# Low sums and the small products among them as two column halves of the TensorE array

## The chip, the cores and the metric

The kernel runs on one NeuronCore of a Trainium2 chip. The metric is the device time of one execution in microseconds; each time given for a kernel is a median over several runs. A profile is one execution recorded by the hardware profiler: every instruction of every engine has its start and duration, and the waits between engines are inferred from semaphores. The engines are named PE (TensorE matmuls), PEld (TensorE weight loads), DVE (VectorE), ACT (ScalarE), POOL (GpSimd) and SP (SyncE, which issues most transfers).

## The reference

One block of a perceiver: cross attention of 32 x 64 queries on 32 contexts of 1601 keys, then a recurrent mixing of the 64 positions, then a feed-forward layer, each on the layer-normed input and each added to it. All in float32.

```python
def xattn(query, context, w_q, w_kv, w_out, b_out):      # 16 heads of 64
    q = query @ w_q                                      # 256 -> 1024
    k, v = split(context @ w_kv)                         # 192 -> 2 x 1024
    attn = softmax(q k^T * 64**-0.5)                     # per head, 64 x 1601
    return (attn v) @ w_out + b_out

def mixing(x, ...):
    k, v, r = k_in @ Wk.T, v_in @ Wv.T, sigmoid(r_in @ Wr.T)   # inputs mixed with the shifted x
    wkv = scan over time of (num + e*v) / (den + e)
    return (r * wkv) @ Wo.T + bo

x = x + xattn(layernorm(x), ctx_768, ...)
x = x + mixing(layernorm(x), ...)
x = x + relu(layernorm(x) @ w1 + b1) @ w2 + b2           # 256 -> 1024 -> 256
```

## The kernel before, in words

**Folding.** The key and value weights are never applied to the context. In a setup part (up to about 140 us) the queries are multiplied by the key weights, so that a score is a product of 192 context channels with a folded query; the folded queries go through DRAM (`q_dram`). The value weights are applied after the sums over the keys (`Out.vproj`). A context of 1601 keys is 12 chunks of 128 keys and one of 65 (`KC` = 12, `KR` = 65, `NCK` = 13), and has 192 channels: 128 "low" ones and 64 "high" ones (`C2` = 64).

**Halves.** The attention loop runs over `u` = 0 to 63: 32 contexts, each with two halves of 8 heads (8 x 64 = 512 columns, `HALF`). For each half PE does, in this order:

- `scores(u)`: for each chunk three products with 64 channels each (L466), where the chunks go in pairs: one uses array rows 0 to 63, the other rows 64 to 127, so that two matmuls of 64 rows x 128 columns run at once (row pairs). The last chunk's 65 keys are done in L485, with 256 moving columns a matmul.
- `av_lo` of the half before (`last`): the low sums. 13 matmuls (L569) with the 128 low channels of a chunk as the weights (128 rows x 128 columns, the whole array) and the 512 columns of exponentials as the moving operand, all added in one PSUM tile `o_lo`. After some of the chunks a list `fill` puts in other work:
  - phase 1 (every fourth half): `Out.yproj` after chunk 2 (8 matmuls, L642, tile `y_ps`, 256 moving columns) and `Mixing.out` of an earlier tile after chunk 6 (2 matmuls, L444, `ry`);
  - phase 2: `Mixing.mix` after chunk 6, with two 128 x 128 transposes on PE (L361, `xT_ln`);
  - phase 3: `Mixing.project` after chunk 3 (Wk and Wv, four matmuls each, L383 in `proj`) and `Mixing.gate` after chunk 9 (Wr, four more).
- `Out.vproj` in phase 0: value weights, 64 columns a matmul (L629, `v_ps`), two heads in the two column halves of the array.
- `av_hi`: the high sums. The weights are the 64 high channels of a chunk, so a matmul needs 64 columns of the array; even chunks use columns 0 to 63 and odd ones columns 64 to 127, and their sums stay apart in the two partition halves of `o_hi` (12 matmuls in L583, two more for the 65 keys in L593, with 256 moving columns each). Which column half a matmul uses follows from the partitions of its output: `self.ph[o * C2 : (o + 1) * C2, :]`.

A matmul in float32 leaves two records in the trace, each with a weight load of its own, so 832 matmuls of the low sums (64 halves x 13) are 1664 records.

Meanwhile ACT copies scores out of PSUM (L473) and takes exponentials (L514), DVE takes maxima (L477), subtracts them (L513), adds the exponentials up (L540) and transposes the next context (L260), and POOL reduces over partitions (L503, L546). No planner sets the order: PE executes its instructions as the loop issues them.

**After the loop** the last half's sums are done with `older.project` and `older.gate` as fill, then `vproj`, `yproj`, and the feed-forward part: transposes of the normed rows (L749), `h_ps` (L761) and `fy` (L775) over four blocks of 512 rows, all with the whole array. Among the first two blocks' matmuls stand the rest of the last two mixing tiles: `older.out` (L444), `mixer.mix` (L361), `mixer.project` and `mixer.gate` (L383), `mixer.out` (L444).

Of the kernel before, what the change touches and what calls it, by code (L numbers as in the profile page):

```python
# [15 lines left out]
P = 128  # L16
# [4 lines left out]
def kernel(  # L21
# [35 lines left out]
    nc = tc.nc  # L57
# [59 lines left out]
    with ExitStack() as st_b:  # L117
        with ExitStack() as st_a:
# [218 lines left out]
            ps_s = st_a.enter_context(tc.tile_pool(name="ps_s", bufs=2, space=PSUM))  # L337
            ps_o = st_a.enter_context(tc.tile_pool(name="ps_o", bufs=1, space=PSUM))

            def bank(shape, name):  # L340
                return ps_m.tile(shape, F32, tag="m", name=name)

            class Mixing:
# [13 lines left out]
                def mix(self):  # L357
                    i = self.i
                    pt = bank([P, 2, 2, T], f"xT_ln2_{i}")
                    for c in range(2):  # L360
                        nc.tensor.transpose(pt[:, c, :, :], self.xn[:, c * P : (c + 1) * P], ident)  # L361
                    xp = rp.tile([P, 2, 2, T + 1], F32, tag="xp", name=f"xp_{i}")
                    nc.gpsimd.memset(xp[:, :, :, 0:1], 0.0)
                    nc.scalar.copy(xp[:, :, :, 1 : T + 1], pt)
                    self.mixed = []
                    for n, nm in enumerate(("k", "v", "r")):
                        tmp = rp.tile([P, 2, 2, T], F32, tag="e", name=f"tmp_{nm}_{i}")
                        mi = rp.tile([P, 2, 2, T], F32, tag=f"in_{nm}", name=f"in_{nm}_{i}")
                        for c in range(2):
                            nc.scalar.activation(  # L370
                                tmp[:, c], xp[:, c, :, 0:T], AF.Copy, scale=omm[:, n, c : c + 1]
                            )
                            nc.vector.scalar_tensor_tensor(
                                mi[:, c], xp[:, c, :, 1 : T + 1], cols[:, 2 + n, c : c + 1],
                                tmp[:, c], ALU.mult, ALU.add,
                            )
                        self.mixed.append(mi.rearrange("p c b t -> p c (b t)"))

                def proj(self, n, w):
                    ps = bank([P, 2, 2, T], f"{w}_ps_{self.i}")  # L380
                    for c in range(2):
                        for hc in range(2):
                            nc.tensor.matmul(  # L383
                                ps[:, c, :, :],
                                lhsT=rw_T[w][:, hc, c * P : (c + 1) * P],
                                rhs=self.mixed[n][:, hc, :],
                                start=(hc == 0),
                                stop=(hc == 1),
                            )
                    return ps  # L390
# [49 lines left out]
                def out(self):  # L440
                    i = self.i
                    py = bank([P, D], f"ry_{i}")
                    for c in range(2):
                        nc.tensor.matmul(  # L444
                            py,
                            lhsT=self.rw[:, c, :],
                            rhs=rw_T["Wo"][:, c, :],
                            start=(c == 0),
                            stop=(c == 1),
                        )  # L450
                    nc.vector.tensor_tensor(x_sb[:, i, :], x_sb[:, i, :], py, ALU.add)
                    nc.vector.tensor_tensor(
                        x_sb[:, i, :], x_sb[:, i, :], bias_rows[:, 1, :], ALU.add
                    )
# [65 lines left out]
            class Half:  # L520
# [43 lines left out]
                def av_lo(self, fill):  # L564

                    self.po = ps_o.tile([P, HALF], F32, tag="o_lo", name=f"o_lo_{self.u}")
                    for c in range(NCK):
                        n = P if c < KC else KR
                        nc.tensor.matmul(  # L569
                            self.po,  # L570
                            lhsT=self.ctx[0:n, self.at[c], 0:P],
                            rhs=self.s_sb[0:n, c, :],
                            start=(c == 0),
                            stop=(c == NCK - 1),
                        )
                        for work in fill.get(c, ()):
                            work()
# [36 lines left out]
            class Out:  # L614
# [23 lines left out]
                def yproj(self):  # L638
                    i = self.i
                    py = bank([P, D], f"y_ps_{i}")  # L640
                    for k in range(NP):
                        nc.tensor.matmul(  # L642
                            py,
                            lhsT=self.outT[:, k, :],
                            rhs=wo_sb[:, k, :],
                            start=(k == 0),
                            stop=(k == NP - 1),
                        )
                    nc.vector.tensor_tensor(x_sb[:, i, :], x_sb[:, i, :], py, ALU.add)
                    nc.vector.tensor_tensor(  # L650
                        x_sb[:, i, :], x_sb[:, i, :], bias_rows[:, 0, :], ALU.add
                    )
# [5 lines left out]
            for u in range(2 * B):  # L658
                b, j = divmod(u, 2)

                phase, i = (u - 5) % 4, (u - 5) // 4
                out, mixer, older = outs[max(i, 0)], mixers[max(i, 0)], mixers[max(i - 1, 0)]
                fill = {}
                if phase == 1 and i >= 0:
# [46 lines left out]
            older, mixer, out = mixers[NT - 2], mixers[NT - 1], outs[NT - 1]  # L711
# [138 lines left out]
```

## Time and profile before

| | |
|---|---|
| median of 3 runs | 2626.44 us (2626.01 to 2626.71) |
| the profiled execution, its own time | 2624.3 us |
| its span | 2622.5 us |
| granted TensorE clock, mean | 0.997 |
| PE busy | 2593.2 us, 99% |
| DVE busy | 1907.2 us, 73% |
| ACT busy | 953.6 us, 36% |
| DMA, mean share of the 16 engines in queue q1 | 32.9% |
| attention loop, low sums first at | 186 us, last at 2485 us |

How to read the profile's lines: a group is a line of the kernel, an engine and an operation, the tiles "out<-in", the rows*columns of the array and partitions x moving columns of the operand, the number of records, then busy time in all, mean ns of one, and the idle time ahead of them. Matmuls are pipelined: a record lasts longer than the distance to the next one, so busy time of a group divided by its count, or the distance of starts, tells the rate, not the mean duration. In a timeline a line gives start, duration, engine, line, operation and the number of records merged in it.

### The profile page before, as it was taken

The page shows a single profiled execution, that of the slowest core. Times are in us where ns is not written, and L with a number is a line of the kernel's source. Part 1 is how long each engine was busy: PE and PEld are TensorE (multiplying, and loading weights), DVE is VectorE, ACT ScalarE, POOL GpSimd, SP SyncE. Part 2 cuts the span into 40 slices and gives each one's busy share as a digit, 9 for nine tenths or more (in the row PEclk, how much of TensorE's full clock was granted, in tenths as well). Part 3 has the DMA queues.
Part 4 walks back from the last instruction along what each step waited for, and adds up shares of the span by engine and source line. Part 5 has one row for each costly group of instructions (what it writes and reads, how often), then busy time and mean ns, then how long its engine had stood idle before and what let it go on. Part 6 is the DMA issues. An engine that isn't in the chain of part 4 may idle for free.

```text
span 2622.5 us, 28521 instructions
## 1 busy us (share of the span) xinstructions
PE 2593.2 (99%) x11456; PEld 1217.1 (46%) x11456; DVE 1907.2 (73%) x2283; ACT 953.6 (36%) x1019; POOL 355.3 (14%) x176
## 2 busy tenths in 40 slices
PE   8989999999999999999999999999999999999999
PEld 3334444444444444444444444444444444444466
DVE  4458878777787878777787868777787868787741
ACT  2333334333333334343433333343433334343221
POOL 0011111111111111111111111111111111111100
PEclk9989999999999999999999999999999999999999
DMA  8983333233322323333331313333331323310100
GB/s 202 284 162 57 56 51 63 44 63 63 63 57 49 63 39 63 44 63 63 63 63 44 63 39 63 46 61 63 63 63 44 63 45 57 59 29 20 51 11 23
DMA packets 437781, 169.33 MB, mean 65 GB/s; under 512 B 332400, under 2 KB 423952, under 8 KB 437648
## 3 DMA queue, kind: packets, MB, share of 16 engines
q1 hardware_dynamic: 437104, 166.46, 32.9%
q8 instruction: 90, 1.47, 0.3%
q10 hardware_dynamic: 544, 1.05, 0.1%
q14 instruction: 43, 0.35, 0.0%
HBM read 138.60 MB, written 27.26 MB: 63 GB/s over the span
## 4 chain that ended last, share of the span: by engine, by line
PE 96%; DMA 2%; SPq 1%; DVE 1%; POOL 0%; issue 0%; ACT 0%; DVEq 0%; POOLq 0%; ACTq 0%
PE s_ps L466 37%; PE o_lo L569 28%; PE o_hi L583 13%; PE s_ps_r L485 3%; PE fy L775 2%; PE v_ps L629 2%; PE y_ps L642 2%; PE h_ps L761 2%; PE q_ps L195 2%; PE o_hi L593 1%; PE ql_ps L211 1%; DMA q_dram<-q_lo 1%; PE Wv_ps L383 1%; PE Wr_ps L383 1%; PE Wk_ps L383 1%; DMA q_dram<-q_hi 1%
## 5 line engine op out<-in xcount | busy, mean ns | idle before, releaser
L466 PE MATMUL s_ps<-q,cT 64*128 64x512 f32 x4608 | 1011.3, 594 | 8.6 <-ACT s_sb L473 7.8
L569 PE MATMUL o_lo<-s_sb,c 128*128 128x512 f32 (+1 forms) x1664 | 743.5, 596 | 0.0
L473 ACT COPY s_sb<-s_ps 128x1024 f32<-128x1024 f32 x384 | 388.6, 1012 | 958.6 <-PE s_ps L466 945.5
L466 PEld LDWEIGHTS s_ps<-q,cT 64*128 64x128 f32 x4608 | 442.6, 188 | 548.9 <-issue 537.9
L514 ACT ACTIVATE s_sb<-s_sb 128x2048 f32<-128x2048 f32 (+1 forms) x256 | 398.6, 1585 | 466.0 <-DVE s_sb L513 466.0
L513 DVE TENSOR_TENSOR s_sb<-s_sb,mb 128x2048 f32<-128x2048 f32 (+1 forms) x256 | 471.6, 1886 | 101.9 <-POOL mb L503 101.9
L569 PEld LDWEIGHTS o_lo<-s_sb,c 128*128 128x128 f32 (+1 forms) x1664 | 307.5, 190 | 358.1 <-issue 350.8
L477 DVE TENSOR_TENSOR m<-m,s_sb 128x1024 f32<-128x1024 f32 x256 | 313.6, 1225 | 180.1 <-ACT s_sb L473 168.2
L583 PE MATMUL o_hi<-s_sb,c 128*64 128x512 f32 x1536 | 342.9, 595 | 0.0
L546 POOL PARTITION_ALL_REDUCE den<-sum x64 | 207.4, 3240 | 834.9 <-DVE oT L609 673.2
L540 DVE TENSOR_TENSOR t<-t,s_sb 128x1024 f32<-128x1024 f32 x256 | 310.5, 1213 | 4.0
L503 POOL PARTITION_ALL_REDUCE mb<-mx x64 | 114.2, 1785 | 906.7 <-DVE mx L496 788.7
L583 PEld LDWEIGHTS o_hi<-s_sb,c 128*64 128x64 f32 x1536 | 105.3, 137 | 220.0 <-issue 197.2
L556 DVE STREAM_TRANSPOSE turned<-den 128x512 f32<-128x512 f32 x64 | 45.5, 711 | 221.3 <-POOL den L546 221.3
L485 PE MATMUL s_ps_r<-q,cT 64*65 64x256 f32 x768 | 93.6, 376 | 0.0
L260 DVE STREAM_TRANSPOSE cT<-cb 128x768 f32<-128x768 f32 x96 | 92.7, 967 | 0.0
L475 DVE TENSOR_TENSOR m<-s_sb 128x1024 f32<-128x1024 f32 x64 | 75.8, 1184 | 10.3 <-ACT s_sb L473 10.3
L485 PEld LDWEIGHTS s_ps_r<-q,cT 64*65 64x65 f32 x768 | 54.0, 134 | 52.8 <-issue 33.5
L538 DVE TENSOR_TENSOR t<-s_sb 128x1024 f32<-128x1024 f32 x64 | 77.5, 1211 | 0.0
L102 POOL TENSOR_TENSOR rstd_ln<-rstd_ln,root 128x1 f32<-128x1 f32 (+1 forms) x24 | 31.3, 1304 | 276.5 <-DVE rstd_ln L101 276.5
L195 PE MATMUL q_ps<-xnT,wq_sb 128*128 128x512 f32 x128 | 61.0, 616 | 0.0
L642 PE MATMUL y_ps<-wo_sb,outT 128*128 128x256 f32 x256 | 58.0, 379 | 0.0
(111 smaller groups left out, 1507.4 us busy)
## 6 DMA issues: line engine op xcount, KB each, us to landing
q<-q_dram SPq DMA_DIRECT2D x64, 768.0 KB, 6.6
c<-in_ctx_dram SPq DMA_DIRECT2D x32, 1152.0 KB, 6.2
cb<-in_ctx_dram SPq DMA_DIRECT2D x192, 104.0 KB, 4.2
cb<-in_ctx_dram SPq DMA_DIRECT2D x192, 96.0 KB, 3.3
q_dram<-q_lo SPq DMA_DIRECT2D x16, 1024.0 KB, 8.6
q_dram<-q_hi SPq DMA_DIRECT2D x32, 256.0 KB, 6.8
x_sb<-in_x_dram SPq DMA_DIRECT2D x4, 512.0 KB, 9.7
w_sb<-in_L_ffn_w_dram SPq DMA_DIRECT2D x2, 1024.0 KB, 5.0
```

The lines of the kernel that those rows point to most:

```text
L195: nc.tensor.matmul(pq, lhsT=wq_sb[:, c, hp * P : (hp + 1) * P], rhs=xnT[:, c, :], start=(c == 0), stop=(c == 1),)
L466: nc.tensor.matmul(ps[:, k, :], lhsT=cT[rs, s, i * P : (i + 1) * P], rhs=q[rs, s, js : js + HALF], start=(s == 0), stop=(s == NS - 1),)
L473: nc.scalar.copy(s_sb[:, 2 * i : 2 * i + 2, :], ps)
L477: nc.vector.tensor_tensor(m2, m2, s_sb[:, 2 * i : 2 * i + 2, :], ALU.max)
L485: nc.tensor.matmul(ps[0:KR, k, 0:HH], lhsT=cT[rs, s, NB1 * BL : KT + 1], rhs=q[rs, s, js + k * HH : js + (k + 1) * HH], start=(s == 0), st ...
L503: nc.gpsimd.partition_all_reduce(mb, mx, P, bass_isa.ReduceOp.max)
L513: nc.vector.tensor_tensor(s, s, m, ALU.subtract)
L514: nc.scalar.activation(s, s, AF.Exp)
L540: nc.vector.tensor_tensor(t2, t2, p[:, 2 * i : 2 * i + 2, :], ALU.add)
L546: nc.gpsimd.partition_all_reduce(self.den, self.sum, P, bass_isa.ReduceOp.add)
L569: nc.tensor.matmul(self.po, lhsT=self.ctx[0:n, self.at[c], 0:P], rhs=self.s_sb[0:n, c, :], start=(c == 0), stop=(c == NCK - 1),)
L583: nc.tensor.matmul(self.ph[o * C2 : (o + 1) * C2, :], lhsT=self.ctx[:, self.at[c], P:C], rhs=self.s_sb[:, c, :], start=(c < 2), stop=False ...
```

## The change

A helper beside `bank` in the attention part splits one matmul of 128 output partitions in two of 64: the same moving operand, half of the weights' columns each, and the two partition halves of the same output.

```diff
+            def matmul(out, lhsT, rhs, start, stop):
+
+                for o in range(2):
+                    rs = slice(o * P // 2, (o + 1) * P // 2)
+                    nc.tensor.matmul(
+                        out[rs], lhsT=lhsT[:, rs], rhs=rhs, start=start, stop=stop,
+                        skip_group_check=True,
+                    )
```

It is called in place of `nc.tensor.matmul` in four places, with nothing else changed there:

```diff
 (Mixing.proj, L383)
-                            nc.tensor.matmul(
+                            matmul(
                                 ps[:, c, :, :],
 (Mixing.out, L444)
-                        nc.tensor.matmul(
+                        matmul(
                             py,
 (Half.av_lo, L569)
-                        nc.tensor.matmul(
+                        matmul(
                             self.po,
 (Out.yproj, L642)
-                        nc.tensor.matmul(
+                        matmul(
                             py,
```

The transposes, the scores, `vproj`, the high sums and the feed-forward matmuls stay as they are.

## The prediction

> **What bounds the kernel now.** I read the page's busy shares, clock row and chain first.
>
> ```profile
> PE 2593.2 (99%) x11456; PEld 1217.1 (46%) x11456; DVE 1907.2 (73%) x2283; ACT 953.6 (36%) x1019; POOL 355.3 (14%) x176
> ...
> PEclk9989999999999999999999999999999999999999
> ...
> PE 96%; DMA 2%; SPq 1%; DVE 1%; POOL 0%; issue 0%; ACT 0%; DVEq 0%; POOLq 0%; ACTq 0%
> ```
>
> TensorE is busy nearly throughout at its full granted clock, and 96% of the chain that ended last is PE. In the view of the waits all of PE's waits add to 24.4 us, and none lies between 180 and 2474 us. So in the attention loop time leaves the span only where PE's own records come closer together; VectorE, the next engine, has 27% to spare.
>
> Next the groups by line, with shapes kept apart.
>
> ```profile
> L569 PE MATMUL o_lo<-s_sb,c 128*128 128x512 f32 x1536 | 688.5, 597 | 0.0
> ...
> L583 PE MATMUL o_hi<-s_sb,c 128*64 128x512 f32 x1536 | 342.9, 595 | 0.0
> ```
>
> The low sums (L569) use all 128 columns and take 688.5 / 1536 = 448 ns a record. The high sums (L583) use 64 columns, two matmuls in the two column halves at once: 342.9 / 1536 = 223 ns a record, 446 a pair. Each matmul of the program leaves two records (64 halves x 13 = 832 matmuls, 1664 records of L569). So whole array and column pair already work at one rate. Inside a run the starts are 429 ns apart for both; a pair's second record starts 7 ns after its first. Column tiles therefore promise nothing in steady state; the question is the seams. Three arrangements follow each other in every half: row pairs (scores, L466 and L485), whole array (L569 and what is put among it), column pairs (L629, L583, L593). The timeline shows the seam from whole to columns:
>
> ```profile
> 1288.98 0.19 PEld L569 LDWEIGHTS o_lo<-s_sb,c 65*128 65x128 f32 x1 [0.24 <-issue]
> 1289.41 0.19 PEld L569 LDWEIGHTS o_lo<-s_sb,c 65*128 65x128 f32 x1 [0.24 <-issue]
> 1290.36 0.20 PEld L583 LDWEIGHTS o_hi<-s_sb,c 128*64 128x64 f32 x4 [0.76 <-issue]
> ...
> 1290.84 0.14 PEld L583 LDWEIGHTS o_hi<-s_sb,c 128*64 128x64 f32 x2 [0.29 <-issue]
> ```
>
> Within a run a load goes out beside the matmul before it, every 0.43. At the seam it doesn't: the last low record starts at 1289.84, so the next was due at 1290.27, but load and matmul come together at 1290.36 (0.09 late), and the second pair comes 0.48 instead of 0.43 later (0.05, the first load of 64 columns that nothing covers). The record starts give 91 + 51 = 142 ns; all 64 ends of low sums (49 into L583, 15 into L629) lie within 1 ns of each part. The seam from row pairs to whole:
>
> ```profile
> 1278.47 0.38 PE L485 MATMUL s_ps_r<-q,cT 64*65 64x256 f32 x2
> 1278.78 0.70 PE L569 MATMUL o_lo<-s_sb,c 128*128 128x512 f32 x1
> ...
> 1279.32 0.19 PEld L569 LDWEIGHTS o_lo<-s_sb,c 128*128 128x128 f32 x1 [0.24 <-issue]
> ```
>
> L485's pairs are 0.216 apart, so 1278.68 was due: 0.10 late, and the next start is 0.53 instead of 0.43 later, 0.10 for a load of 128 columns. The records: 98 + 104 ns, 63 times. Where the arrangement stays, the seam is free even if line and tile change:
>
> ```profile
> 1217.58 0.39 PE L629 MATMUL v_ps<-oT,wv_hi 128*64 128x128 f32 x4
> 1217.80 0.60 PE L583 MATMUL o_hi<-s_sb,c 128*64 128x512 f32 x2
> ```
>
> Four records of L629 are two pairs of 109 ns, and 0.22 is just that. So are L569 into L642 and back. A switch from columns to whole happens once in the loop's end, from L593 into L569 at 2470.98: 99 + 104.
>
> **The change, part by part.** It makes column pairs of L569, L383, L444 and L642. The transposes of mix (L361) and everything in the feed-forward part stay whole. Arithmetic, transfers, waits and order stay; each of 1664 + 256 + 384 + 64 = 2368 records becomes a pair, two matmuls and two loads more in place of one and one.
>
> 1. The end of the low sums no longer changes arrangement: 64 x 142 ns = 9.09 us less.
> 2. Their beginning goes from row pairs to column pairs, a seam that the trace lacks. The gap is 91 to 99 ns at every clean switch, whichever two arrangements meet (columns to rows 98, whole to columns 91), so I leave its 98. The uncovered load is 51 for 64 columns and 104 for 128; here it is 64, so 53 ns less: 63 x 53 = 3.34 us. If the load stayed at 104, nothing.
> 3. L593 into L569 at 2470.98 (203 ns) and L629 into L642 at 2494.25 (100 + 105) vanish: 0.41 us.
> 4. L383's records are loads of 128 columns with 128 moving columns. From 1316.58 to 1318.36 sixteen take 1.78 us, 111.3 each; L629's pairs, the same work in halves, 3.06 us for 28 (1214.74 to 1217.80), 109.3. 384 x 2.0 = 0.77 us less, bounded by none and by this.
> 5. L642 and L444 move 256 columns at 216 ns. As pairs: L485's pairs take 216, L593's 220. I take 216, since the 4 ns of L593 also stand in L569 whole where its rows go from 128 to 65 (433 for 429); at 220 it would be 320 x 4 = 1.3 us more.
> 6. Mix's two transposes stand among low sums in 15 halves (1284.89 is one), now with no seam. They get two: columns to whole, 98 + 55 (a transpose's load, from 133.38, where L320 follows L226), and back, 91 + 51. 15 x 295 ns = 4.43 us more; between 55 and 104 for that load it is up to 0.74 more.
> 7. In the feed-forward part L444 (twice), L383 (two places) stand among whole-array work, and the transposes L749 follow L642. Nine switches: 153, 142, 153, 142, 202, 142, 204, 142 and 202 ns, 1.48 us. The first three (448 ns) lie ahead of L361 at 2504.64, where PE waits 1.39 us for VectorE's `xn_ln`, which hangs on L642 and not on them; that cover takes them, or costs 0.45 if it is gone. 1.03 us more.
>
> PE's sequencer gets more instructions: a pair has four where there were two. L629 issues four in every 109 ns with no gap, and the densest new run, L383, needs the same, so I count none. The Trainium skill ("TensorEngine Tiling (Array Packing)", section "Instruction Overhead") speaks against this, giving each matmul some 60 cycles of overhead; at the 2.4 GHz of its page "TensorE: Matmul & The Clock Gate" 2368 further records in series would be an estimated 59 us more. L629's rows contradict a cost in series.
>
> The sum: 9.09 + 3.34 + 0.41 + 0.77 - 4.43 - 1.03 = 8.15 us less. PE waits for nobody in the loop, so all of it should reach the end; a cycle shrinks by some 0.2 us in 34, and the ACT copies of L473 idle 1.56 us before each, so nothing is late next. The profiled execution took 2624.3 us (span 2622.5); it would be 2616.2. The runs' median is 2.1 above it: 2626.44 - 8.1 = **2618.3 us**, 0.31% less. A measurement of this kernel tells about 0.2% (5.25 us) from no change.
>
> **Rivals.**
>
> - *A pair with one moving operand isn't free.* The halves of L583 read different chunks and those of L629 different heads; the new halves read the same columns at the same moment, which no row shows. If only the 7 ns by which the second starts later added to each pair, 2368 x 7 = 16.6 us more, 2634.9 us, slower. It eats the gain from 3.4 ns a pair, and is slower by over 0.2% from 5.6. If halves ran one after another it would be 1664 x 429 + 384 x 111 + 320 x 216 ns, some 826 us. Against it: 429 ns is the start distance of pair and whole record alike, so the 7 ns are hidden there. Chance 0.11. The Trainium skill ("TensorE: Matmul & The Clock Gate", section "Measured speedup vs the span model") adds about 4 ns per further tile to a pack's span: an estimated 9.5 us more here, 2627.8; the rows of L583 show no such sum in a run of packs.
> - *The entry from row pairs keeps its price* (104 ns, or a longer gap as both directions change), or the switches round mix cost more than the rows. Without step 2 it is 4.8 us less: 2621.6, which is within 0.2%. For it: no row has this seam. Against it: the load's price goes by its columns at every seam seen. Chance 0.15.
> - *The change doesn't do what it says*: the switch into the high sums stays, because the tiles meet there in another way. Without step 1, 0.9 us more: 2627.4. Against it: L629 into L583 is free and its tiles are those of L569 then. Chance 0.09.
>
> **How the numbers follow.** The forecast has 0.65. Range: below, the tail's switches all hidden and a median apart by the runs' 0.7 us, 2616.5; above, step 2 lost (3.3), step 5 at 220 (1.3) and part of steps 4, 6 and 7, 2623.5. That holds the forecast and the second rival, 0.80. Faster by over 0.2%: 0.65 and a third of the second rival, 0.70. Within: the rest of that, the third rival and a mild first, 0.20. Slower: the first, 0.10.
>
> **What would show it.** L583 after L569 with its load 0.43 after the one before and no 0.09; the first low pair 0.31 after L485's last and the next 0.48 later; L569 with twice the records at 223 ns each and loads of 137 ns; about 0.15 before and after L361. Pairs of L569 at 433 or more would prove the first rival; wrong too would be any new wait of PE.

## The result, and the profile after

The changed kernel takes 2616.94 us (median of 6 runs, 2615.43 to 2618.07), the kernel before 2626.55 us beside it; the ratio of the runs is 0.9965 (the two medians alone give 0.9963), 95% interval 0.9955 to 0.9976, so 6.3 to 11.8 us faster. Run again beside other kernels it came out at 0.9965 (0.9953 to 0.9978). The forecast was 2618.3 us, 0.31% less.

The page of after (span 2616.2 us; its own time 2618.07), the same lines as before:

```profile
PE 2588.2 (99%) x13824; PEld 1129.4 (43%) x13824; DVE 1908.3 (73%) x2283; ACT 953.6 (36%) x1019; POOL 356.4 (14%) x176
...
PEclk9989999999999999999999999999999999999999
...
PE 95%; DMA 2%; DVE 1%; SPq 1%; issue 0%; POOL 0%; ACT 0%; DVEq 0%; POOLq 0%; ACTq 0%
```

Nothing has changed hands: PE is still the bound, at the same clock, with 2368 more records (11456 to 13824). The groups by line, shapes apart (the helper's calls all have L344; L583 is now L592):

```profile
L344 PE MATMUL o_lo<-s_sb,c 128*64 128x512 f32 x3072 | 686.6, 595 | 0.0
L592 PE MATMUL o_hi<-s_sb,c 128*64 128x512 f32 x1536 | 340.4, 592 | 0.0
```

686.6 / 3072 is 223.5 ns a record, 447 a pair: the low sums cost in halves what they cost whole (448). The gain stands at their ends. The timeline at the end of the low sums of one half (start, duration, line; PEld are the loads, each beside the matmul before its own):

```profile
591.63 0.14 PEld L344 LDWEIGHTS o_lo<-s_sb,c 65*64 65x64 f32 x2 [0.29 <-issue]
592.07 0.14 PEld L592 LDWEIGHTS o_hi<-s_sb,c 128*64 128x64 f32 x2 [0.29 <-issue]
...
592.50 0.14 PEld L592 LDWEIGHTS o_hi<-s_sb,c 128*64 128x64 f32 x2 [0.29 <-issue]
...
592.93 0.14 PEld L592 LDWEIGHTS o_hi<-s_sb,c 128*64 128x64 f32 x2 [0.29 <-issue]
```

L592's first loads go out beside the last low matmul, and everything is 0.43 apart: the seam is gone. The entry:

```profile
505.40 0.81 PE L494 MATMUL s_ps_r<-q,cT 64*65 64x256 f32 x6
...
506.14 0.20 PEld L344 LDWEIGHTS o_lo<-s_sb,c 128*64 128x64 f32 x4 [0.38 <-issue]
...
506.62 0.14 PEld L344 LDWEIGHTS o_lo<-s_sb,c 128*64 128x64 f32 x2 [0.28 <-issue]
```

Three pairs of 0.216 from 505.40 end at 506.05, so 506.14 is still 0.09 to 0.10 late, but the next start is 0.48 later and no longer 0.53. Where mix's two transposes stand, both switches are new:

```profile
842.13 1.03 PE L344 MATMUL o_lo<-s_sb,c 128*64 128x512 f32 x4
843.09 0.44 PE L370 MATMUL xT_ln<-ident,xn_ln 128*128 128x128 f32 x2
843.46 0.65 PE L344 MATMUL o_lo<-s_sb,c 128*64 128x512 f32 x2
```

Two pairs of 0.43 from 842.13 end at 842.99, and L370 comes 0.10 after that; its two records, 0.22 without seams, hold PE for 0.37.

One measure is used from here on: the time from the first record of the low sums to the end of the span. It is 2436.09 us before (first record at 186.44) and 2428.26 after (187.98): 7.83 us less. The profile of after_again, the same kernel, gives 2428.27, so it repeats far better than the whole time. The part ahead of it executes the same instructions in both kernels, yet in ten profiles the first low sum comes between 185.0 and 191.1 us, in no order by kernel.

### The profile page after: what moved, and what is told of

The parts are those of the page before. It is cut to its first block, busy times and chain, and to the rows that moved or that the text cites. A ratio compares the mean times of both kernels' runs of the same rounds, so it can differ in the third digit from the quotient of the medians.

```text
span 2616.2 us, 33242 instructions
## 1 busy us (share of the span) xinstructions
PE 2588.2 (99%) x13824; PEld 1129.4 (43%) x13824; DVE 1908.3 (73%) x2283; ACT 953.6 (36%) x1019; POOL 356.4 (14%) x176
## 4 chain that ended last, share of the span: by engine, by line
PE 95%; DMA 2%; DVE 1%; SPq 1%; issue 0%; POOL 0%; ACT 0%; DVEq 0%; POOLq 0%; ACTq 0%
PE s_ps L475 38%; PE o_lo L344 28%; PE o_hi L592 13%; PE s_ps_r L494 3%; PE fy L784 2%; PE v_ps L638 2%; PE h_ps L770 2%; PE y_ps L344 2%; PE q_ps L195 1%; DMA q_dram<-q_lo 1%; PE o_hi L602 1%; PE Wk_ps L344 1%; PE Wr_ps L344 1%; PE Wv_ps L344 1%; PE ry L344 1%; SPq L242 0%
## 5 line engine op out<-in xcount | busy, mean ns | idle before, releaser
L475 PE MATMUL s_ps<-q,cT 64*128 64x512 f32 x4608 | 1010.3, 594 | 8.0 <-ACT s_sb L482 7.1
L344 PE MATMUL o_lo<-s_sb,c 128*64 128x512 f32 (+1 forms) x3328 | 741.6, 594 | 0.0
L475 PEld LDWEIGHTS s_ps<-q,cT 64*128 64x128 f32 x4608 | 442.2, 188 | 547.6 <-issue 537.9
L344 PEld LDWEIGHTS o_lo<-s_sb,c 128*64 128x64 f32 (+1 forms) x3328 | 231.1, 137 | 427.4 <-issue 417.7
L592 PE MATMUL o_hi<-s_sb,c 128*64 128x512 f32 x1536 | 340.4, 592 | 0.0
L592 PEld LDWEIGHTS o_hi<-s_sb,c 128*64 128x64 f32 x1536 | 109.3, 136 | 211.3 <-issue 206.1
L344 PE MATMUL y_ps<-wo_sb,outT 128*64 128x256 f32 x512 | 58.0, 379 | 0.0
```

Source lines behind the costliest of these rows:

```text
L344: nc.tensor.matmul(out[rs], lhsT=lhsT[:, rs], rhs=rhs, start=start, stop=stop, skip_group_check=True,)
L475: nc.tensor.matmul(ps[:, k, :], lhsT=cT[rs, s, i * P : (i + 1) * P], rhs=q[rs, s, js : js + HALF], start=(s == 0), stop=(s == NS - 1),)
L592: nc.tensor.matmul(self.ph[o * C2 : (o + 1) * C2, :], lhsT=self.ctx[:, self.at[c], P:C], rhs=self.s_sb[:, c, :], start=(c < 2), stop=False ...
```

## The experiments

| kernel | median us | ratio to before (95%) | first low sum to end: expected, measured |
|---|---|---|---|
| lo_only | 2637.97 | 1.0046 (1.0031 to 1.0061) | 2448.5, 2448.39 |
| small_only | 2646.7 | 1.0081 (1.0067 to 1.0095) | 2457.2, 2457.03 |
| mix_at_entry | 2614.05 | 0.9958 (0.9945 to 0.9970) | 2426, 2426.04 |
| rest_first | 2614.99 | 0.9961 (0.9949 to 0.9974) | 2425.1, 2425.74 |
| tail_whole | 2616.76 | 0.9967 (0.9954 to 0.9979) | 2426.9, 2426.98 |
| all_three | 2610.52 | 0.9945 (0.9932 to 0.9957) | 2421.4 to 2422.2, 2421.96 |
| quarters | 2625.99 | 0.9998 (0.9989 to 1.0007) | 2436 to 2438, 2435.96 |
| after_again | 2616.8 | 0.9965 (0.9953 to 0.9978) | 2428.2, 2428.27 |

The theory is that of the seams. Its main rival is that column tiles are cheaper in themselves, whatever stands around them; the first two kernels undo one part of the change each.

### lo_only: the low sums alone

```diff
 (Mixing.proj, Mixing.out, Out.yproj)
-                            matmul(
+                            nc.tensor.matmul(
```

> Only the low sums in column halves; the small products stay whole. Theory of seams (each change of arrangement costs a gap of 91 to 101 ns and one uncovered load: 51 ns for 64 columns, 104 for 128, 55 for a transpose; inside a run column pairs and whole array go at 429 ns): the gains of steps 1 to 3 stay without the last product's seam (-12.6 us), mix costs 15 x 302 ns = +4.5, and the small products among the low sums are 59 excursions (15 of the output projection, 14 + 30 of the mixing products) of 101 + 104 + 92 + 51 = 347 ns = +20.5. Against before +12.4 us, about 2639, slower by 0.47%; from the first low sum to the end of the span 2448.5 us (before 2436.1, after 2428.2). Rival, column tiles are cheaper in themselves (shorter loads, 137 for 190 ns) and what stands around them doesn't matter: the low sums are 1664 of the 2368 records, so about 70% of the gain of after, -5 to -7 us, about 2620.

It is slower than before. The last gate product of a half, whole again (L392) between low sums in halves:

```profile
886.01 1.46 PE L344 MATMUL o_lo<-s_sb,c 128*64 128x512 f32 x6
887.40 1.16 PE L392 MATMUL Wr_ps<-in_r,Wr_T 128*128 128x128 f32 x8
888.49 1.51 PE L344 MATMUL o_lo<-s_sb,c 128*64 128x512 f32 x6
```

Three pairs of 0.43 from 886.01 end at 887.30, 0.10 before L392; and L392 takes 1.09 to the next low sum where eight whole records take 0.89 without a seam. The parts by record starts are 100 + 104 into whole (the first counted from the start of the pair before), 96 + 51 back, at all 15 gate products. So the same low sums in halves win 8 us or lose 12, by what stands among them, and the rival falls.

### small_only: the small products alone

```diff
 (Half.av_lo)
-                        matmul(
+                        nc.tensor.matmul(
                             self.po,
```

> Only the small products in column halves; the low sums stay whole. Theory of seams: 59 excursions from whole array to columns and back inside the low sums, 347 ns each, +20.5 us; the tail as in after, +1.3; the weight products at 109 instead of 111 ns, -0.7. Against before +21.1 us, about 2647.6, slower by 0.8%; from the first low sum to the end 2457.2 us. With low sums only the two parts would add to +33 us, where both together give -8. Rival, column tiles are cheaper in themselves: the remaining 30% of the gain, -2 to -3 us, about 2624.

The seams are there with the sides exchanged:

```profile
888.09 1.45 PE L578 MATMUL o_lo<-s_sb,c 128*128 128x512 f32 x3
889.47 1.09 PE L344 MATMUL Wr_ps<-in_r,Wr_T 128*64 128x128 f32 x16
890.49 1.55 PE L578 MATMUL o_lo<-s_sb,c 128*128 128x512 f32 x3
```

Eight pairs take 1.02 where 0.87 would do. Taken one at a time, the two halves of the change cost 12.3 and 20.9 us; together they save 7.8. The difference of 41.1 us is what two times 59 excursions cost (2 x 59 x 347 ns = 40.9).

### mix_at_entry: the transposes at a seam that is there anyway

```diff
-                    fill = {6: [mixer.mix]}
+                    fill = {-1: [mixer.mix]}
 (av_lo, ahead of the chunks)
+                    for work in fill.get(-1, ()):
+                        work()
```

> The changed kernel, with the two transposes of mix issued ahead of the low sums' first chunk instead of after chunk 6, at a seam that is there anyway. Theory of seams: rows to whole to columns is 98 + 55 + 94 + 51 = 298 ns where rows to columns is 149, so the mix costs 149 ns instead of 302: 15 x 153 = 2.3 us less than after; from the first low sum to the end about 2426 (after 2428.2). Rival, the transposes cost by themselves (their 165 ns to the second one) wherever they stand: same as after.

2.22 us less than after, as expected. Half of what the transposes cost in after was their place; at the seam that is there anyway they still cost 149 ns (97 + 55 + 94 + 51, where 97 + 51 stood without them).

### rest_first: a first load of 65 columns

```diff
 (scores: the block of the last 65 keys, L485 to its copy, ahead of the loop over chunks)
+                HH = HALF // 2
+                ps = ps_s.tile([P, 2, HALF], F32, tag="s", name=f"s_ps_{u}_r")
+                ...
                 for i in range(KC // 2):
...
-                HH = HALF // 2
-                ps = ps_s.tile([P, 2, HALF], F32, tag="s", name=f"s_ps_{u}_r")
```

> The changed kernel, with the scores of the last 65 keys done first in each half instead of last, so that the first load after the switch from columns to rows has 65 columns and not 128. Theory of seams (the uncovered load goes by its columns): 104 to about 53 ns at 62 seams, 3.1 us less than after; the exit from rows keeps its 98 ns. Rival, the price of a switch is one of the switch and not of the load: the 104 ns stay and the time is that of after.

```profile
527.65 0.60 PE L602 MATMUL o_hi<-s_sb,c 65*64 65x256 f32 x4
528.18 1.08 PE L475 MATMUL s_ps_r<-q,cT 64*65 64x256 f32 x8
```

The gap stays (L602's two pairs of 0.22 end at 528.09, and L475 starts 0.09 after that); the load behind it falls from 104 to 52 ns at all 62 places, and the scores of a half from 16.946 to 16.893 us. 62 x 52 = 3.2 us would follow; 2.52 came, since the scores of one half near 209 us lasted 0.74 longer, where PE waited for a score copy of ACT (0.5 of it in the waits). So a switch has two prices: the gap, which nothing changed here, and the load, which goes by its columns.

### tail_whole and all_three

```diff
-            def matmul(out, lhsT, rhs, start, stop):
+            def matmul(out, lhsT, rhs, start, stop, halves=True):
+                if not halves:
+                    nc.tensor.matmul(out, lhsT=lhsT, rhs=rhs, start=start, stop=stop)
+                    return
 (proj)
+                                halves=self.i < NT - 1,
 (Mixing.out)
+                            halves=i < NT - 2,
```

> The changed kernel, with the mixing products that fall into the feed-forward part (those of the last tile, and the last but one's output product) whole as before. Theory of seams: the switches after the output projection go but for one, 0.9 us up to the first record of fy and 0.45 behind it: 1.3 us less than after, 2426.9 from the first low sum to the end (after 2428.2). Rival, these products lie beside waits for VectorE and cost nothing: same as after.

1.28 us less than after in the profile; the medians, with the part ahead of the loop in them, can't tell it (2616.76 and 2616.8).

> The changed kernel with the three edits together: mix ahead of the low sums, the last 65 keys' scores first, the tail's products whole. Theory of seams: the savings add, 2.2 + 2.5 to 3.3 + 1.3 = 6.0 to 6.8 us less than after, 2421.4 to 2422.2 from the first low sum to the end, ratio to before about 0.9945. Rival, another engine becomes the bound as PE's cycle shrinks: less than the sum, and new waits of PE for ACT or VectorE inside the loop.

6.30 us less than after, and from 200 us to the loop's end the view of the waits has none of PE. At 0.9945 (2610.52 us) it beats both kernels.

### quarters: four column tiles

```diff
-                for o in range(2):
-                    rs = slice(o * P // 2, (o + 1) * P // 2)
+                for o in range(4):
+                    rs = slice(o * P // 4, (o + 1) * P // 4)
```

> The changed kernel with four column tiles of 32 instead of two of 64 in the helper. Theory of seams: the distance of starts stays 429 ns for 512 columns, as the later starts inside a group are hidden; the seam into the high sums and value products is back, 64 x (91 to 105 + 51) = 9.1 to 10.0 us, and a first load of 32 columns takes about 26 ns less at 63 entries, -1.6: about 8 us more than after, 2436 to 2438 from the first low sum to the end. Rival, each further tile adds its later start (7 ns) to the group: two more per record, 2368 x 14 = 33 us more. Open for both: whether eight instructions in 109 ns still issue in the weight products.

```profile
435.34 1.06 PE L344 MATMUL Wk_ps<-in_k,Wk_T 128*32 128x128 f32 x32
436.21 1.06 PE L344 MATMUL Wv_ps<-in_v,Wv_T 128*32 128x128 f32 x32
437.08 2.33 PE L344 MATMUL o_lo<-s_sb,c 128*32 128x512 f32 x20
```

32 records, eight groups of four, take 0.87: 109 ns a group, as with two tiles. Groups of the low sums are 429 ns apart though their starts are spread over 20. Inside a run neither the later starts nor eight instructions in 109 ns cost anything. Yet the kernel stands where before stood, because the seam into the high sums is back: the loads of L592 come at 592.64 with the first matmul, 520 ns after the last start among the low sums, where after has 422.

```profile
592.64 0.20 PEld L592 LDWEIGHTS o_hi<-s_sb,c 128*64 128x64 f32 x4 [0.84 <-DVE num L431]
```

(The releaser in brackets is only the last that the profile knows; PE itself idles nowhere here.) All 64 of these seams have 91 + 51 ns counted from the last start of the group, as whole to halves did. But the group's first record lies 20 ns ahead of its last, so by the distance of groups the gap is 111: the later starts, hidden inside a run, are paid at its exit. Against after the seams cost 10.4 us and the narrower first loads (24 for 51 ns) give back 1.7. In the loop that makes 8.6 us. The total is 7.70 us more than after, just under the forecast, because of something that the theory doesn't have: from the last value product to the first record of fy this kernel takes 0.92 us less than after. The instructions of the tail stand in yet another order there, and PE doesn't wait for the transposes of mix (L370).

### after_again

> The changed kernel once more beside the others, for the size of its gain. Theory of seams: 7.8 us from the first low sum to the end, the part ahead of it the same but for chance, so 0.9965 to 0.9975. Rival, the part ahead of the loop got shorter too: a ratio under 0.996.

Its ratio fits the theory's range and not the rival's, but the interval reaches both.

## Why the prediction was right, point by point

| step | forecast us | found in the records |
|---|---|---|
| 1, end of the low sums | -9.09 | 64 seams of 142 ns gone: -9.09 |
| 2, entry | -3.34 | load 51 for 104, gap the same, at 63 entries: -3.36 |
| 3, two single seams | -0.41 | both gone from PE's records, but the second lies ahead of PE's wait at L370: -0.20 reached the end |
| 4, weight products | -0.77 | pairs 109.2 apart for 111.7, and the record behind each product 2.5 ns sooner: -0.96 |
| 5, output products | 0 | pairs 216 apart: 0 |
| 6, mix | +4.43 | 101 + 56 + 94 + 51 = 302 ns, of which 3 stood there before: +4.48 |
| 7, tail | +1.03 | six switches behind the wait +1.04; L370 itself 0.29 later: +1.33 |
| sum | -8.15 | -7.83 measured; the rows make -7.8 |

The mechanism was that of the prediction: the gain comes from the seams, each at the price read off the kernel before, and the work between the seams costs what it did. Steps 1, 2, 5 and 6 held to the size, and step 4 gave 0.2 us more, its 2.0 ns a record being 2.5. That the total is off by only 0.3 us is in part luck: steps 3 and 7 together were 0.5 us off, and step 4 made up 0.2 of it.

**The terms that were mis-sized are step 7 and the second seam of step 3**, both at one place: PE's wait for `xn_ln` ahead of the transposes of mix (L361 before, L370 after). The prediction said that the wait hangs on L642 and would cover the three switches ahead of it, and that the order stays. The tail before, then after (start, duration, line):

```profile
2497.81 0.60 PE L749 MATMUL xT_ln<-ident,xn_ln 128*128 128x128 f32 x4
2498.24 1.03 PE L444 MATMUL ry<-Wo_T,rwv 128*128 128x256 f32 x4
2499.11 0.63 PE L749 MATMUL xT_ln<-ident,xn_ln 128*128 128x128 f32 x4
...
2504.64 0.44 PE L361 MATMUL xT_ln<-ident,xn_ln 128*128 128x128 f32 x2 [1.39 <-DVE xn_ln L353]
```

```profile
2490.14 0.66 PE L758 MATMUL xT_ln<-ident,xn_ln 128*128 128x128 f32 x4
2490.73 1.08 PE L344 MATMUL ry<-Wo_T,rwv 128*64 128x256 f32 x6
2491.74 0.65 PE L758 MATMUL xT_ln<-ident,xn_ln 128*128 128x128 f32 x4
2492.32 0.65 PE L344 MATMUL ry<-Wo_T,rwv 128*64 128x256 f32 x2
2492.90 3.70 PE L770 MATMUL h_ps<-xT,w_sb 128*128 128x512 f32 x8
2497.38 0.44 PE L370 MATMUL xT_ln<-ident,xn_ln 128*128 128x128 f32 x2 [0.78 <-DVE xn_ln L362]
```

L344's output product is torn: its last half (x2) stands behind the next transposes. That makes five switches ahead of L370 in place of three, and four records that run alone instead of as two pairs, 1.1 us more for PE in all. The cover took all of it: PE still waits 0.78 us at L370. Two other things cost time there. First, the wait hides savings as well as costs. The 0.20 us that L629 into L642 no longer takes (step 3) lie ahead of it and never reach the end. tail_whole shows this: that seam is gone there too, and yet the transposes start 10.61 us after the last value product, as before (10.60); the wait takes up the difference (1.44 us for 1.39, with one new switch of 0.16 ahead of it).

So the wait doesn't hang on L642. Second, in after `xn_ln` itself comes 0.29 us later (L370 starts 10.90 us after the last value product), since VectorE's instructions stand in another order. Before, then after:

```profile
2502.67 0.15 DVE L101 TENSOR_SCALAR rstd_ln<-mv_ln 128x1 f32<-128x1 f32 x1
2503.66 0.41 DVE L741 TENSOR_SCALAR xn_ln<-x_sb,mv_ln,rstd_ln 128x256 f32<-128x256 f32 x1 [0.84 <-POOL rstd_ln L102]
```

```profile
2495.66 0.41 DVE L750 TENSOR_SCALAR xn_ln<-x_sb,mv_ln,rstd_ln 128x256 f32<-128x256 f32 x1 [0.77 <-POOL rstd_ln L102]
2495.98 0.15 DVE L101 TENSOR_SCALAR rstd_ln<-mv_ln 128x1 f32<-128x1 f32 x1
```

A step of the layer norm ahead of mix (L101) now comes behind a row of the feed-forward part's (L750), where before it came ahead of it (L741). In tail_whole, without halves in the tail, it is ahead again. The four profiles with these products whole have the transposes 10.60 to 10.61 us after the last value product, the five with them in halves 10.90 to 10.91. So halving the tail's products changed the order of the instructions around them. That the loop's issue alone sets the order, as said ahead of the prediction, does not hold in this part: the source has all eight transposes of the first block ahead of `older.out`, and already before L444 stands between them. What sets the order there the runs don't show.

**The first rival** (a pair with one moving operand isn't free) is refuted at its own price: L344's low pairs are 429 ns apart, and quarters with three later starts as well. The Trainium skill ("TensorE: Matmul & The Clock Gate", section "Measured speedup vs the span model") adds some 4 ns per further tile; in a stream of packs these runs show 0, and 7 ns for a second tile once, at the exit from the stream. Nor did the 2368 further records cost anything in series: the rows above make up the measured time without them. **The second** is refuted by the entries, 51 ns of load at all 63. **The third** by the free seam at 592.07; quarters shows what it would have looked like.

**What stays open.** The medians moved by 9.6 us (by the ratio 9.2), the part from the first low sum on by 7.8 in the profiles. The rest, 1.4 to 1.8 us, is not explained. The profiles don't show it ahead of the first low sum, where the instructions are the same: that record comes at 186.44 before and at 187.98 and 185.74 in the two profiles of after, and single executions differ there by up to 6 us. The intervals hold 7.8 too. So how close the median came to the forecast (1.4 us) says less than the rows do.

## What to carry to other kernels

On a TensorE that is busy nearly throughout, look at the records next to each change of tiling, not at the share of busy time: a switch had a price (here 0.14 to 0.2 us between whole, rows and halves) while the tilings inside a run had the same rate. So give neighbours one tiling, even where a product would fill the whole array: halves were worth it here because nearly all that stands among them was halved too (the transposes that stayed whole cost 4.5 us), and one half of the change alone was a loss. What can't be converted goes to a switch that exists already, and the first load after a switch should be the narrowest. A wait for another engine hides the savings that lie ahead of it as it hides the costs.

## What the runs showed of the hardware

- Every switch of tiling costs a gap of 89 to 96 ns, whichever tilings meet: rows, whole, halves or quarters of the columns. It is counted from the time at which the next record was due after the last one before the switch (429 ns with 512 moving columns, 216 with 256, 109 with 128), and holds at every switch without a wait behind the first low sum in the ten profiles. Counted from the first record of a pack, as above, it is 7 ns more for two tiles and 20 for four. The Trainium skill ("TensorEngine Tiling (Array Packing)", section "Key Properties") says that changing the mode, not just the tile, drains the array; by that rule these gaps are its price here, and going on to another tile or line in one mode cost at most 4 ns in the loop.
- Behind the gap comes one load that nothing covers: 24 ns for 32 columns, 51 for 64, 52 for 65, 104 for 128. The Trainium skill ("TensorE: Matmul & The Clock Gate", section "LDWEIGHTS (loading the stationary operand)") gives columns / 1.2 ns, 27, 53, 54 and 107, and these runs agree within 3 ns. The transposes are an exception: their loads have 128 columns too and cost 55 to 58 ns, about half of that; here the measurement decides.
- Four tiles of 32 columns start 7 ns apart and still keep 109 ns a group with 128 moving columns.
